# A last transpose moved from TensorE to DRAM, an earlier start and a closer order in a four-layer graph kernel

## Chip, cores and metric

One core of a Trainium2 chip. The metric is the device time of one execution in microseconds; every kernel here was run several times beside runs of the kernel before on the same chip. The experiments ran on three chips in turn, on which the kernel before took 1467.11, 1466.91 and 1466.23 us; so times from different groups may be compared to about 1 us. In the text PE is TensorE, DVE is VectorE, ACT is ScalarE, POOL is GpSimd and SP is SyncE, as in the profile.

## The reference, cut to what matters

```python
x = layernorm(x + attention_over_neighbours_0(x, adj, ...))      # layer 0
x = layernorm(x + attention_over_neighbours_1(x, adj, ...))      # layer 1
# layer 2: five gated steps; adj is symmetric and serves as both matrices
def step(h, _):
    m = einsum('nm,bmd->bnd', adj, h)                 # needs h with the nodes on the partitions
    u3 = h @ u3_w.T + u3_b                            # needs h with the features on the partitions
    z = sigmoid(av @ w3_w.T + w3_b + u3)              # av = [m, m]
    r = sigmoid(av @ w4_w.T + w4_b + u3)
    hv = tanh(av @ w5_w.T + w5_b + (r * h @ u5_w.T + u5_b))
    return (1 - z) * h + z * hv, None
x = layernorm(x + scan(step, x, length=5))
x = layernorm(x + chebyshev_3(x, adj, weight_1))                 # layer 3
```

`x` is 64 graphs x 256 nodes x 128 features, all float32. The kernel works on 32 units of two graphs.

Of the kernel before, what the change touches and what calls it, by code (L numbers as in the profile page):

```python
# [13 lines left out]
P = 128  # L14
# [6 lines left out]
BL = 32  # L21
NEAR = 1
DIRECT = 2


class Cell:
# [17 lines left out]
class Plan:  # L44
# [2 lines left out]



    LATENCY = {"pe": 700, "dve": 600, "act": 600, "pool": 700, "sp": 4000}  # L50
    OWN = {"pe": 0, "dve": 70, "act": 70, "pool": 100}

    def __init__(self, banks):
        self.free_banks = list(banks)
        self.tasks = []
        self.unit, self.step, self.layer = -1, 0, 0

    def add(self, eng, ns, fn, reads=(), writes=(), after=(), wait=0, group=None, dma=False):
        t = Task(eng, ns, fn, self.unit, wait, dma or eng == "sp")
        for c in reads:  # L60
            t.deps.update(c.writers)
            c.readers.append(t)
        for c in writes:
            if c.bank and not c.writers:
                t.takes.append(c)
            if group is None or c.group is not group:
                c.waits = {*c.writers, *c.readers} - {t}
                c.writers, c.readers, c.group = [], [], group
            t.deps.update(c.waits)
            c.writers.append(t)  # L70
        t.deps.update(after)
        t.deps.discard(t)
        for c in {id(c): c for c in (*reads, *writes) if c.bank}.values():
            c.users += 1
            t.banks.append(c)
        t.step = self.step = self.step + 1
        t.layer = self.layer
        self.tasks.append(t)
        return t

# [3 lines left out]
    def run(self, spawn, units, key):  # L84
# [32 lines left out]
        while any(ready.values()) or running:  # L117

            for t in [t for t in running if t.end <= now]:
                running.remove(t)  # L120
                for c in t.banks:
                    c.users -= 1
                    if not c.users:
                        self.free_banks.append(c.ap)
                open_units[t.unit] -= 1
                if not open_units[t.unit] and t.unit in lane_of:
                    start(lane_of[t.unit])
            for e, tasks in ready.items():
                if free[e] > now:
                    continue  # L130
                fit = [t for t in tasks if t.at <= now and len(t.takes) <= len(self.free_banks)]
                if not fit:
                    continue
                t = min(fit, key=key)
                tasks.remove(t)
                for c in t.takes:
                    c.ap = self.free_banks.pop(0)
                order.append(t)
                free[e] = t.off = now + t.ns
                t.end = t.off + self.LATENCY["sp" if t.dma else e] + t.wait  # L140
                done_at[t] = t.end
                running.append(t)
                for n in t.then:
                    n.left -= 1
                    n.at = max(n.at, self.seen_at(t, n))
                    if not n.left:
                        ready[n.eng].append(n)
            times = [t.end for t in running] + [f for f in free.values() if f > now]
            times += [t.at for tasks in ready.values() for t in tasks if t.at > now]
            times = [x for x in times if x > now]  # L150
            if not times:
                assert not any(ready.values()), "the plan is stuck"
                break
            now = min(times)
# [5 lines left out]
def kernel(  # L160
# [45 lines left out]
    def cell(name, shape):  # L206
        return Cell(sb(name, shape))
# [8 lines left out]
        return n * (cols * 1.667 + 5)  # L216


    def load(name, src, shape, ns=450):
        c = cell(name, shape)  # L220
        add("sp", ns, lambda: nc.sync.dma_start(c.ap, src), (), (c,))
        return c

    x_u = x.rearrange("(u b) (c p) d -> u p b c d", b=UB, p=P)
# [3 lines left out]

    zs = [cell(f"z{k}", [P, T]) for k in range(LANES)]

    def load_x(u):
        z = zs[u % LANES]
        if u < LANES:
            add("sp", 1000, lambda: nc.sync.dma_start(z.ap.rearrange("p (b c d) -> p b c d", b=UB, c=NC), x_u[u]), (), (z,))
            return
        parts = object()
        for a in range(D // BL):
            add("sp", 540, lambda a=a: nc.sync.dma_start(
                z.ap[a * BL : (a + 1) * BL].rearrange("j (b i) -> j b i", i=BL),
                x_a[u, a].rearrange("(b j) i -> j b i", j=BL)), (), (z,), group=parts)  # L240

    w1 = load("w1", W, [D, D])
    asd = cell("asd", [D, 2])
    for k, a in enumerate((a_src, a_dst)):
        add("sp", 450, lambda k=k, a=a: nc.sync.dma_start(asd.ap[:, k : k + 1], a), (), (asd,), group=asd)
    wo = load("wo", others_weight, [D, D])
    att = load("att", att_weight.rearrange("(k d) o -> d (k o)", k=2), [D, 2])
    load_x(0)
    wself = load("wself", self_weight, [D, D])
    adj_t = load("adj_t", adj.rearrange("(c p) j -> p c j", p=P), [P, NC, N])  # L250
    load_x(1)
    load_x(2)
    gates = [load(f"gate{k}", w.rearrange("o (s d) -> o s d", s=2), [D, 2, D])
             for k, w in enumerate((w3_w, w4_w, w5_w))]
    u3 = load("u3", u3_w, [D, D])
    u5 = load("u5", u5_w, [D, D])
    biases = cell("biases", [D, 5])
    for k, b in enumerate((w3_b, w4_b, w5_b, u3_b, u5_b)):
        add("sp", 450, lambda k=k, b=b: nc.sync.dma_start(biases.ap[:, k : k + 1], b.rearrange("(p o) -> p o", o=1)),
            (), (biases,), group=biases)  # L260
    load_x(3)
    wk = load("wk", weight_1, [D, D, 7], 1500)
    for u in range(4, LANES):
        load_x(u)


# [23 lines left out]
    for mc in range(NC):  # L290
# [2 lines left out]
                ps_adj.ap[:, mc * N + ic * P : mc * N + (ic + 1) * P], adj_t.ap[:, ic, mc * P : (mc + 1) * P], ident.ap),  # L293
                (adj_t, ident), (ps_adj,))
    add(ACT, 500, lambda: nc.scalar.copy(adjT.ap.rearrange("p c n -> p (c n)"), ps_adj.ap), (ps_adj,), (adjT,))

    adjTp, adj_p = cell("adjTp", [P, NC, N]), cell("adj_p", [P, NC * NC, BL, P // BL])
    add(DVE, 600, lambda: nc.vector.tensor_copy(
        adj_p.ap, adj_t.ap.rearrange("p i (m q j) -> p (i m) j q", m=NC, j=BL)), (adj_t,), (adj_p,))
    ps_adjp = bank()  # L300
    for mc in range(NC):
        for ic in range(NC):
            add(PE, 110, lambda mc=mc, ic=ic: nc.tensor.transpose(
                ps_adjp.ap[:, mc * N + ic * P : mc * N + (ic + 1) * P],
                adj_p.ap[:, ic * NC + mc].rearrange("p j q -> p (j q)"), ident.ap), (adj_p, ident), (ps_adjp,))
    add(ACT, 500, lambda: nc.scalar.copy(adjTp.ap.rearrange("p c n -> p (c n)"), ps_adjp.ap), (ps_adjp,), (adjTp,))
    neg0 = cell("neg0", [P, NC, N])
    add(DVE, 420, lambda: nc.vector.tensor_scalar(neg0.ap, adjT.ap, 0.0, NEG, op0=ALU.is_le, op1=ALU.mult),
        (adjT,), (neg0,))

    top0 = cell("top0", [P, NC])
    add(DVE, 350, lambda: nc.vector.tensor_reduce(top0.ap, neg0.ap[:, :, P:N], AX.X, ALU.max), (neg0,), (top0,))

    mask1 = cell("mask1", [P, NC, N])
    add(DVE, 420, lambda: nc.vector.tensor_copy(mask1.ap, adjT.ap), (adjT,), (mask1,))
    for c in range(NC):
        add(DVE, 250, lambda c=c: nc.vector.tensor_add(
            mask1.ap[:, c, c * P : (c + 1) * P], adjT.ap[:, c, c * P : (c + 1) * P], ident.ap),
            (adjT, ident, mask1), (mask1,))
    add(DVE, 420, lambda: nc.vector.tensor_scalar(mask1.ap, mask1.ap, 0.0, None, op0=ALU.is_gt), (mask1,), (mask1,))  # L320


    centre = cell("centre", [P, P])
    add(DVE, 150, lambda: nc.vector.tensor_scalar_add(centre.ap, ident.ap, -1.0 / D), (ident,), (centre,))
# [33 lines left out]
        add(DVE, 230, lambda t=t, n=n, ps=ps: nc.vector.tensor_copy(t.ap, ps.ap[:, 0:n]), (ps,), (t,))  # L358


    gs = [cell(f"gs{k}", [D, D]) for k in range(3)]
    for k in range(3):
        add(DVE, 250, lambda k=k: nc.vector.tensor_add(gs[k].ap, gates[k].ap[:, 0, :], gates[k].ap[:, 1, :]),
# [9 lines left out]
    add(DVE, 150, lambda: nc.vector.tensor_scalar_mul(bias2.ap[:, 0:2], bias2.ap[:, 0:2], 0.5), (bias2,), (bias2,))  # L373


    w3 = cell("w3", [D, 2, 2, D])
    add(DVE, 250, lambda: nc.vector.tensor_add(w3.ap[:, 0, 0, :], wk.ap[:, :, 0], ident.ap), (wk, ident), (w3,))
    for k in range(1, 4):
# [5 lines left out]
    for mc in range(NC):  # L384
        for kc in range(NC):
            add(PE, mm_ns(N), lambda mc=mc, kc=kc: nc.tensor.matmul(
                ps_a2.ap[:, mc * N : (mc + 1) * N], adj_t.ap[:, kc, mc * P : (mc + 1) * P], adjT.ap[:, kc, :],
                start=(kc == 0), stop=(kc == NC - 1)), (adj_t, adjT), (ps_a2,))
    add(DVE, 600, lambda: nc.vector.tensor_copy(a2T.ap.rearrange("p c n -> p (c n)"), ps_a2.ap), (ps_a2,), (a2T,))


    def lane_cells(k):
# [269 lines left out]
    def layer2(u, L):  # L662
        h, ht = turned(u, L), X[u]
        for step in range(STEPS):
# [39 lines left out]
            if step < STEPS - 1 and far(u):  # L704
# [8 lines left out]
                for a in range(D // BL):  # L713
# [2 lines left out]
                        L["hb"].ap[a * BL : (a + 1) * BL].rearrange("j (q g i) -> (j q) g i", g=G, i=BL)),  # L716
                        (L["hb"],), (ht,), group=parts)
                continue
            ps_t = bank()
            for g in range(G):  # L720
                add(PE, 110, lambda g=g, h=h, ps_t=ps_t: nc.tensor.transpose(  # L721
# [1 line left out]
            if step < STEPS - 1:  # L723
                add(ACT, 500, lambda ps_t=ps_t: nc.scalar.copy(L["ht"].ap, ps_t.ap), (ps_t,), (ht,))
        y = L["m"]
        add(DVE, 600, lambda: nc.vector.tensor_add(y.ap, ps_t.ap, X[u].ap.rearrange("p b c d -> p (b c d)")),
            (ps_t, X[u]), (y,))
        layernorm(u, L, y_pairs(y))


# [29 lines left out]
    def spawn(u, lane):  # L760
        for k, layer in enumerate((layer0, layer1, layer2, layer3)):
            plan.layer = k
            layer(u, lanes[lane])
            if not k and u + LANES < NU:
                load_x(u + LANES)



    def first(t):
        late = t.unit - (NU - LANES)  # L770
        if late >= 0 and t.layer > 1:
            return (1, t.step + late * LEAD)
        return (0, t.unit - (LANES if t.layer < 2 and t.unit >= LANES else 0))
# [34 lines left out]
```

## The kernel before: what the change touches

The kernel is written as a list of tasks. Each task names an engine, a duration that its author assumes (`ns`), what it reads and what it writes. A small planner then plays the program through with assumed durations and assumed latencies, and the order in which it picks the tasks becomes the order of instructions on each engine. The chip executes each engine's instructions in exactly that order. Seven units are in flight at a time, each in its own set of buffers, a "lane".

```python
LANES = 7
...
    LATENCY = {"pe": 700, "dve": 600, "act": 600, "pool": 700, "sp": 4000}     # assumed, ns
...
    # Plan.run: whenever an engine is free, among the tasks whose inputs have (by the plan) arrived
                t = min(fit, key=key)
                order.append(t)
                free[e] = t.off = now + t.ns
                t.end = t.off + self.LATENCY["sp" if t.dma else e] + t.wait
...
    def first(t):                                   # the key: the oldest unit first
        late = t.unit - (NU - LANES)
        if late >= 0 and t.layer > 1:
            return (1, t.step + late * LEAD)
        return (0, t.unit - (LANES if t.layer < 2 and t.unit >= LANES else 0))
```

The state `h` of a gated step is computed with the features on the partitions. After each step it must be turned. For 29 of the 32 units ("far" ones) the first four steps do that with a DVE transpose of 32x32 blocks and a trip through DRAM that moves the blocks; the last step uses four PE transposes for all units.

```python
            if step < STEPS - 1 and far(u):
                add(DVE, 600, lambda h=h, v=v: nc.vector.transpose(...), (h,), (v,))      # 32x32 blocks
                add("sp", 560, lambda v=v: nc.sync.dma_start(L["hb"].ap, v.ap), (v,), (L["hb"],))
                ...                                                   # four loads hb -> ht
                continue
            ps_t = bank()
            for g in range(G):
                add(PE, 110, lambda g=g, h=h, ps_t=ps_t: nc.tensor.transpose(
                    ps_t.ap[:, g * P : (g + 1) * P], h.ap[:, g * P : (g + 1) * P], ident.ap), (h, ident), (ps_t,))
            ...
        y = L["m"]
        add(DVE, 600, lambda: nc.vector.tensor_add(y.ap, ps_t.ap, X[u].ap...), (ps_t, X[u]), (y,))
```

The softmax here doesn't subtract the row's maximum and nothing guards it: scores larger than these inputs give would overflow.

## Time and profile before

| | kernel before |
|---|---|
| time, median of 3 | 1464.49 us (1464.2 to 1466.8) |
| profiled span | 1463.0 us, granted clock 0.992 |
| PE transposes of L721 | 176 of 128 columns, of them 116 in the last step of far units |
| DMA traffic | 126.90 MB |

These are the waits of PE in the full stretch from 100 to 1400 us of the kernel before: engine and line waiting, what it waited for, us in total, times, longest.

```profile
PE ps L678 <- ACT m L674: 3.6, 3, 1.8
PE ps L678 <- DVE xT L700: 3.1, 2, 1.9
PE ps L658 <- DMA ht<-hb: 1.5, 2, 1.3
```

The full list, two smaller waits included, comes to nine us of 1300. L678 is the gated products and L658 the product with the adjacency.

### The profile page before, as it was taken

How to read it: one execution, taken by the hardware profiler on the slowest of the kernel's cores; microseconds unless marked ns; L12 is line 12 of the kernel's file. 1: busy time of each engine (PE TensorE's matmuls, PEld its weight loads, DVE VectorE, ACT ScalarE, POOL GpSimd, SP SyncE). 2: the span in 40 equal slices, each digit the busy share in tenths (PEclk: the TensorE clock that was granted, in tenths of full speed). 3: DMA queues.
4: the chain of work that ended last, by engine and by line, in shares of the span. 5: the costliest groups of instructions: out<-in, count | busy, mean ns of one | idle time of the engine just before them, and what ended most of it. 6: DMA issues, size and time to landing. Idle time of an engine off the chain costs nothing.

```text
span 1463.0 us, 18345 instructions
## 1 busy us (share of the span) xinstructions
PE 1431.2 (98%) x5733; PEld 967.9 (66%) x5733; DVE 1101.1 (75%) x2569; ACT 723.2 (49%) x1372; POOL 146.2 (10%) x134
## 2 busy tenths in 40 slices
PE   7899999999999999999999999999999999999998
PEld 6666666666667766577666666676666766665667
DVE  6884778868769788777886778977976877767565
ACT  4664446446354465444554545535554554544431
POOL 0110101100011101001010011111100100001011
PEclk9899999999999999999999999999999999999999
DMA  6211243453534444534435344344343334443212
GB/s 148 46 37 22 65 96 86 95 110 78 116 80 95 104 98 87 118 74 99 104 80 108 78 109 100 84 92 107 72 98 85 89 89 99 93 101 70 46 44 65
DMA packets 495280, 126.90 MB, mean 87 GB/s; under 512 B 443856, under 2 KB 465104, under 8 KB 495184
## 3 DMA queue, kind: packets, MB, share of 16 engines
q1 hardware_dynamic: 495184, 125.73, 38.7%
q8 instruction: 46, 0.75, 0.2%
q14 instruction: 50, 0.41, 0.1%
HBM read 71.41 MB, written 54.25 MB: 86 GB/s over the span
## 4 chain that ended last, share of the span: by engine, by line
PE 93%; DVE 3%; ACT 2%; DMA 1%; issue 0%; SPq 0%; DVEq 0%; ACTq 0%
PE ps L678 45%; PE ps L658 22%; PE ps L747 8%; PE ps L754 4%; PE ps L620 3%; PE ps L590 3%; PE ps L523 2%; PE ps L634 2%; PE ps L585 2%; PE ps L721 1%; ACT e L609 1%; PE ps L430 0%; DVE e L554 0%; DVE st L483 0%; DMA rowu<-cu 0%
## 5 line engine op out<-in xcount | busy, mean ns | idle before, releaser
L678 PE MATMUL ps<-m,gT 128*128 128x512 f32 x960 | 460.9, 593 | 3.6 <-ACT m L674 3.6
L678 PEld LDWEIGHTS ps<-m,gT 128*128 128x128 f32 x960 | 177.7, 190 | 152.8 <-issue 126.4
L488 POOL TENSOR_TENSOR rstd<-ve,nhalf 128x4 f32<-128x4 f32 x128 | 145.5, 1139 | 1311.5 <-DVE ve L485 1268.9
L658 PE MATMUL ps<-adjTp,ht 128*128 128x256 f32 x928 | 231.7, 381 | 1.8 <-DMA ht<-hb 1.5
L658 PEld LDWEIGHTS ps<-adjTp,ht 128*128 128x128 f32 x928 | 174.5, 191 | 74.4 <-issue 50.1
L697 DVE TENSOR_TENSOR p<-p,xT 128x512 f32<-128x512 f32 x160 | 109.6, 686 | 95.3 <-ACT p L691 95.0
L674 ACT COPY m<-ps 128x512 f32<-128x512 f32 x160 | 93.4, 584 | 174.0 <-PE ps L658 170.1
L684 ACT ACTIVATE e<-ps,bias 128x512 f32<-128x512 f32 x160 | 109.8, 686 | 133.9 <-PE ps L678 133.8
L693 ACT ACTIVATE e<-ps,bias 128x512 f32<-128x512 f32 x160 | 109.7, 686 | 117.0 <-PE ps L678 116.7
L678 PE MATMUL ps<-xT,gT 128*128 128x512 f32 x320 | 161.4, 594 | 3.1 <-DVE xT L700 3.1
L686 DVE SCALAR_TENSOR_TENSOR e<-e,xT 128x512 f32<-128x512 f32 x160 | 109.2, 684 | 72.4 <-ACT e L684 70.9
L678 PE MATMUL ps<-e,u5T 128*128 128x512 f32 x320 | 161.9, 592 | 0.0
L691 ACT ACTIVATE p<-ps,bias 128x512 f32<-128x512 f32 x160 | 109.7, 686 | 77.9 <-PE ps L678 74.0
L658 PE MATMUL ps<-adjT,x 128*128 128x256 f32 x512 | 132.2, 383 | 0.0
L658 PEld LDWEIGHTS ps<-adjT,x 128*128 128x128 f32 x512 | 95.8, 192 | 42.6 <-issue 32.0
L698 DVE SCALAR_TENSOR_TENSOR p<-e,p 128x512 f32<-128x512 f32 x160 | 109.5, 685 | 2.8 <-ACT e L693 0.4
L700 DVE SCALAR_TENSOR_TENSOR xT<-p,xT 128x512 f32<-128x512 f32 x160 | 109.5, 685 | 2.0
L483 DVE BATCH_NORM_STATS2 st<-ps 128x6 f32<-128x256 f32 x128 | 53.7, 426 | 57.5 <-PE ps L754 38.9
L678 PEld LDWEIGHTS ps<-e,u5T 128*128 128x128 f32 x320 | 59.2, 190 | 51.1 <-issue 40.7
L609 ACT ACTIVATE e<-m,esd 128x256 f32<-128x256 f32 x120 | 87.0, 761 | 2.1 <-DMA m<-row 2.1
L678 PEld LDWEIGHTS ps<-xT,gT 128*128 128x128 f32 x320 | 59.1, 190 | 41.8 <-issue 31.0
L708 DVE STREAM_TRANSPOSE p<-xT 128x512 f32<-128x512 f32 x116 | 81.6, 705 | 1.4
(135 smaller groups left out, 1861.2 us busy)
## 6 DMA issues: line engine op xcount, KB each, us to landing
hb<-p SPq DMA_DIRECT2D x174, 256.0 KB, 2.1
ht<-hb SPq DMA_DIRECT2D x464, 64.0 KB, 2.5
m<-row SPq DMA_DIRECT2D x60, 256.0 KB, 3.7
xT<-hb SPq DMA_DIRECT2D x232, 64.0 KB, 2.5
out_dram<-x SPq DMA_DIRECT2D x32, 256.0 KB, 2.4
z<-in_x_dram SPq DMA_DIRECT2D x100, 64.0 KB, 2.4
z<-in_x_dram SPq DMA_DIRECT2D x7, 256.0 KB, 4.2
u<-rowu SPq DMA_DIRECT2D x60, 3.8 KB, 3.0
```

Of the source, the lines that this page charges most:

```text
L488: add(POOL, 1050, lambda: nc.gpsimd.tensor_tensor(rstd.ap, ve.ap, nhalf.ap, op=ALU.pow), (ve, nhalf), (rstd,))
L609: add(ACT, 600, lambda g=g, b=b: nc.scalar.activation(e.ap[:, g, :].rearrange("p (c n) -> p c n", c=NC), ev()[:, b], AF.Prelu, bias=esd.ap ...
L658: add(PE, mm_ns(N), lambda b=b, mc=mc: nc.tensor.matmul(ps.ap[:, b * N : (b + 1) * N], lhs(b, mc), mat.ap[:, mc, :], start=(mc == 0), stop ...
L678: add(PE, mm_ns(T), lambda: nc.tensor.matmul(ps.ap, w(), rhs.ap, start=start, stop=stop, skip_group_check=True), (c, rhs), (ps,))
L684: add(ACT, 600, lambda ps_g=ps_g: nc.scalar.activation(r.ap, ps_g.ap, AF.Tanh, bias=bias2.ap[:, 1:2], scale=0.5), (ps_g, bias2), (r,))
L686: add(DVE, 600, lambda h=h: nc.vector.scalar_tensor_tensor(r.ap, r.ap, 1.0, h.ap, op0=ALU.add, op1=ALU.mult), (r, h), (r,))
L691: add(ACT, 600, lambda ps_v=ps_v: nc.scalar.activation(v.ap, ps_v.ap, AF.Tanh, bias=bias2.ap[:, 2:3]), (ps_v, bias2), (v,))
L693: add(ACT, 600, lambda ps_g=ps_g: nc.scalar.activation(z.ap, ps_g.ap, AF.Tanh, bias=bias2.ap[:, 0:1], scale=0.5), (ps_g, bias2), (z,))
L697: add(DVE, 600, lambda h=h: nc.vector.tensor_sub(v.ap, v.ap, h.ap), (v, h), (v,))
L698: add(DVE, 600, lambda: nc.vector.scalar_tensor_tensor(v.ap, z.ap, 1.0, v.ap, op0=ALU.add, op1=ALU.mult), (v, z), (v,))
L700: add(DVE, 600, lambda h=h, new=new: nc.vector.scalar_tensor_tensor(new.ap, v.ap, 0.5, h.ap, op0=ALU.mult, op1=ALU.add), (v, h), (new,))
L747: add(PE, mm_ns(N), lambda k=k, src=src, c=c, b=b: nc.tensor.matmul(view(c)[:, :, b, :], bn(src.ap)[:, b, c * P : (c + 1) * P], w3.ap[:, k ...
```

## The change

Its intent has three parts, called here the last step (L), the start (S) and the closer order (C).

L: the last step's state of a far unit also goes through DRAM, in natural token order, and the final addition reads it from SBUF.

```diff
+            if far(u):
+                add(DVE, 600, lambda h=h, v=v: nc.vector.transpose(...), (h,), (v,))
+                parts = object()
+                for a in range(D // BL):
+                    add("sp", 560, lambda a=a, v=v: nc.sync.dma_start(
+                        L["hb"].ap.rearrange("(q j) (a r) -> a j q r", j=BL, a=D // BL)[a],
+                        v.ap[a * BL : (a + 1) * BL].rearrange("j (q r) -> j q r", q=P // BL)), (v,), (L["hb"],), group=parts)
+                add("sp", 450, lambda: nc.sync.dma_start(ht.ap, L["hb"].ap), (L["hb"],), (ht,))
+                continue
             ps_t = bank()
...
-        add(DVE, 600, lambda: nc.vector.tensor_add(y.ap, ps_t.ap, X[u]...), (ps_t, X[u]), (y,))
+        if far(u):
+            add(DVE, 600, lambda: nc.vector.tensor_add(y.ap..., ht.ap..., X[u].ap...), (ht, X[u]), (y,))
+        else:
+            add(DVE, 600, lambda: nc.vector.tensor_add(y.ap, ps_t.ap, X[u]...), (ps_t, X[u]), (y,))
```

S: first loads in another order, the adjacency and unit 1's input issued from ACT; constants that the first unit doesn't need are moved behind those that it does, with a rank in the key; and the first prefetches get a rank. The durations assumed for some first loads change with it (1000 and 1500 ns become 600).

```diff
     w1 = load("w1", W, [D, D])
+    adj_t = load("adj_t", adj.rearrange("(c p) j -> p c j", p=P), [P, NC, N], by=ACT)
+    load_x(0)
+    wo = load("wo", others_weight, [D, D])
...
-    adj_t = load("adj_t", adj.rearrange("(c p) j -> p c j", p=P), [P, NC, N])
-    load_x(1)
+    load_x(1, ACT)
...
+    plan.rank = 0        # ... R2, R3 for groups of constants; u + LANES for prefetches
...
+        if t.rank is not None:
+            return (0, t.rank)
```

C: the planner assumes shorter latencies, still shorter ones in the first 35 us.

```diff
-    LATENCY = {"pe": 700, "dve": 600, "act": 600, "pool": 700, "sp": 4000}
+    LATENCY = {"pe": 500, "dve": 400, "act": 400, "pool": 500, "sp": 4000}
+    EARLY = {"pe": 250, "dve": 180, "act": 200, "pool": 250, "sp": 2500}
...
-                t.end = t.off + self.LATENCY["sp" if t.dma else e] + t.wait
+                t.end = t.off + (self.EARLY if now < START else self.LATENCY)["sp" if t.dma else e] + t.wait
```

More of the change, by code (lines that the diff above doesn't have):

```diff
@@ L23 @@
 DIRECT = 2
+START = 35e3
+R2 = 1
+R3 = 1.5
 class Cell:
@@ L56, in __init__ @@
         self.unit, self.step, self.layer = -1, 0, 0
+        self.rank = None
     def add(self, eng, ns, fn, reads=(), writes=(), after=(), wait=0, group=None, dma=False):
@@ L77, in add @@
         t.layer = self.layer
+        t.rank = self.rank
         self.tasks.append(t)
@@ L216, in mm_ns, with load @@
         return n * (cols * 1.667 + 5)
-    def load(name, src, shape, ns=450):
+    def load(name, src, shape, ns=450, by="sp"):
         c = cell(name, shape)
-        add("sp", ns, lambda: nc.sync.dma_start(c.ap, src), (), (c,))
+        queue = {"sp": nc.sync, ACT: nc.scalar}[by]
+        add(by, ns, lambda: queue.dma_start(c.ap, src), (), (c,), dma=True)
         return c
@@ L229, with load_x @@
     zs = [cell(f"z{k}", [P, T]) for k in range(LANES)]
-    def load_x(u):
+    def load_x(u, by="sp"):
         z = zs[u % LANES]
         if u < LANES:
-            add("sp", 1000, lambda: nc.sync.dma_start(z.ap.rearrange("p (b c d) -> p b c d", b=UB, c=NC), x_u[u]), (), (z,))
+            queue = {"sp": nc.sync, ACT: nc.scalar}[by]
+            add(by, 600, lambda: queue.dma_start(z.ap.rearrange("p (b c d) -> p b c d", b=UB, c=NC), x_u[u]), (), (z,), dma=True)
             return
@@ L245 @@
         add("sp", 450, lambda k=k, a=a: nc.sync.dma_start(asd.ap[:, k : k + 1], a), (), (asd,), group=asd)
-    wo = load("wo", others_weight, [D, D])
     att = load("att", att_weight.rearrange("(k d) o -> d (k o)", k=2), [D, 2])
-    load_x(0)
     wself = load("wself", self_weight, [D, D])
-    adj_t = load("adj_t", adj.rearrange("(c p) j -> p c j", p=P), [P, NC, N])
-    load_x(1)
+    load_x(1, ACT)
     load_x(2)
@@ L256 @@
     u5 = load("u5", u5_w, [D, D])
+    load_x(3)
     biases = cell("biases", [D, 5])
@@ L260 @@
             (), (biases,), group=biases)
-    load_x(3)
-    wk = load("wk", weight_1, [D, D, 7], 1500)
-    for u in range(4, LANES):
+    load_x(4)
+    wk = load("wk", weight_1, [D, D, 7], 600)
+    for u in range(5, LANES):
         load_x(u)
@@ L295 @@
     add(ACT, 500, lambda: nc.scalar.copy(adjT.ap.rearrange("p c n -> p (c n)"), ps_adj.ap), (ps_adj,), (adjT,))
-    adjTp, adj_p = cell("adjTp", [P, NC, N]), cell("adj_p", [P, NC * NC, BL, P // BL])
-    add(DVE, 600, lambda: nc.vector.tensor_copy(
-        adj_p.ap, adj_t.ap.rearrange("p i (m q j) -> p (i m) j q", m=NC, j=BL)), (adj_t,), (adj_p,))
-    ps_adjp = bank()
-    for mc in range(NC):
-        for ic in range(NC):
-            add(PE, 110, lambda mc=mc, ic=ic: nc.tensor.transpose(
-                ps_adjp.ap[:, mc * N + ic * P : mc * N + (ic + 1) * P],
-                adj_p.ap[:, ic * NC + mc].rearrange("p j q -> p (j q)"), ident.ap), (adj_p, ident), (ps_adjp,))
-    add(ACT, 500, lambda: nc.scalar.copy(adjTp.ap.rearrange("p c n -> p (c n)"), ps_adjp.ap), (ps_adjp,), (adjTp,))
     neg0 = cell("neg0", [P, NC, N])
@@ L312 @@
     add(DVE, 350, lambda: nc.vector.tensor_reduce(top0.ap, neg0.ap[:, :, P:N], AX.X, ALU.max), (neg0,), (top0,))
-    mask1 = cell("mask1", [P, NC, N])
-    add(DVE, 420, lambda: nc.vector.tensor_copy(mask1.ap, adjT.ap), (adjT,), (mask1,))
-    for c in range(NC):
-        add(DVE, 250, lambda c=c: nc.vector.tensor_add(
-            mask1.ap[:, c, c * P : (c + 1) * P], adjT.ap[:, c, c * P : (c + 1) * P], ident.ap),
-            (adjT, ident, mask1), (mask1,))
-    add(DVE, 420, lambda: nc.vector.tensor_scalar(mask1.ap, mask1.ap, 0.0, None, op0=ALU.is_gt), (mask1,), (mask1,))
     centre = cell("centre", [P, P])
@@ L358 @@
         add(DVE, 230, lambda t=t, n=n, ps=ps: nc.vector.tensor_copy(t.ap, ps.ap[:, 0:n]), (ps,), (t,))
+    plan.rank = 0
+    mask1 = cell("mask1", [P, NC, N])
+    add(DVE, 420, lambda: nc.vector.tensor_copy(mask1.ap, adjT.ap), (adjT,), (mask1,))
+    for c in range(NC):
+        add(DVE, 250, lambda c=c: nc.vector.tensor_add(
+            mask1.ap[:, c, c * P : (c + 1) * P], adjT.ap[:, c, c * P : (c + 1) * P], ident.ap),
+            (adjT, ident, mask1), (mask1,))
+    add(DVE, 420, lambda: nc.vector.tensor_scalar(mask1.ap, mask1.ap, 0.0, None, op0=ALU.is_gt), (mask1,), (mask1,))
+    plan.rank = R2
     gs = [cell(f"gs{k}", [D, D]) for k in range(3)]
@@ L373 @@
     add(DVE, 150, lambda: nc.vector.tensor_scalar_mul(bias2.ap[:, 0:2], bias2.ap[:, 0:2], 0.5), (bias2,), (bias2,))
+    adjTp, adj_p = cell("adjTp", [P, NC, N]), cell("adj_p", [P, NC * NC, BL, P // BL])
+    add(DVE, 600, lambda: nc.vector.tensor_copy(
+        adj_p.ap, adj_t.ap.rearrange("p i (m q j) -> p (i m) j q", m=NC, j=BL)), (adj_t,), (adj_p,))
+    ps_adjp = bank()
+    for mc in range(NC):
+        for ic in range(NC):
+            add(PE, 110, lambda mc=mc, ic=ic: nc.tensor.transpose(
+                ps_adjp.ap[:, mc * N + ic * P : mc * N + (ic + 1) * P],
+                adj_p.ap[:, ic * NC + mc].rearrange("p j q -> p (j q)"), ident.ap), (adj_p, ident), (ps_adjp,))
+    add(ACT, 500, lambda: nc.scalar.copy(adjTp.ap.rearrange("p c n -> p (c n)"), ps_adjp.ap), (ps_adjp,), (adjTp,))
+    plan.rank = R3
     w3 = cell("w3", [D, 2, 2, D])
@@ L389 @@
     add(DVE, 600, lambda: nc.vector.tensor_copy(a2T.ap.rearrange("p c n -> p (c n)"), ps_a2.ap), (ps_a2,), (a2T,))
+    plan.rank = None
     def lane_cells(k):
@@ L718, in layer2 @@
                 continue
+            if far(u):
+                add(DVE, 600, lambda h=h, v=v: nc.vector.transpose(
+                    v.ap.rearrange("p (q g i) -> p g q i", g=G, i=BL), h.ap.rearrange("p (g q j) -> p g q j", g=G, j=BL)),
+                    (h,), (v,))
+                parts = object()
[5 more added lines that the diff above has]
+                continue
             ps_t = bank()
@@ L725, in layer2 @@
         y = L["m"]
-        add(DVE, 600, lambda: nc.vector.tensor_add(y.ap, ps_t.ap, X[u].ap.rearrange("p b c d -> p (b c d)")),
-            (ps_t, X[u]), (y,))
+        if far(u):
+            add(DVE, 600, lambda: nc.vector.tensor_add(
+                y.ap.rearrange("p (g a i) -> p g a i", g=G, i=BL), ht.ap.rearrange("p (a g i) -> p g a i", g=G, i=BL),
+                X[u].ap.rearrange("p b c (a i) -> p (b c) a i", i=BL)), (ht, X[u]), (y,))
+        else:
+            add(DVE, 600, lambda: nc.vector.tensor_add(y.ap, ps_t.ap, X[u].ap.rearrange("p b c d -> p (b c d)")),
+                (ps_t, X[u]), (y,))
         layernorm(u, L, y_pairs(y))
@@ L764, in spawn @@
             if not k and u + LANES < NU:
+                plan.rank = u + LANES if u < LANES else None
                 load_x(u + LANES)
+                plan.rank = None
     def first(t):
+        if t.rank is not None:
+            return (0, t.rank)
         late = t.unit - (NU - LANES)
```

## The prediction

> **What bounds the kernel now.** I read the page first (busy shares, slices, the chain that ended last), then busy time by stage, then PE's waits, then PE in order of time.
>
> ```profile
> PE 1431.2 (98%) x5733; PEld 967.9 (66%) x5733; DVE 1101.1 (75%) x2569; ACT 723.2 (49%) x1372; POOL 146.2 (10%) x134
> PE   7899999999999999999999999999999999999998
> PE 93%; DVE 3%; ACT 2%; DMA 1%; issue 0%; SPq 0%; DVEq 0%; ACTq 0%
> ```
>
> PE is busy for 98% of the span and makes up 93% of the chain; only the first two slices (and the last) fall short. So time comes off in two ways only: fewer PE instructions, or less time lost before PE is full. A busy PE need not be at its peak, so I did not rest on the share. I took start-to-start distances from the order in time: a 512-column record is 0.43 us after the last, a 256-column one 0.216, a 128-column transpose 0.11. Counting the records of each stage by form and multiplying gives 21.1 us of work in the first 31 us (9.9 lost), 15.6 in 31 to 63 us (16.4 lost), 1378.5 in 63 to 1456.4 (14.9 lost in 1393), and then 6.6 us after the last matmul. Lost time is thus 26 us at the start, about 1% in the middle, and 7 at the end.
>
> ```profile
> 0.00:31.00 31.00, 25.48 (x189) 24.10 (x189) 18.32 (x75) 14.86 (x42) 1.72 (x7) 1.00 0.68 155
> 31.00:63.00 32.00, 21.43 (x115) 18.38 (x116) 31.08 (x106) 17.09 (x51) 5.66 (x5) 0.73 0.31 63
> 100.00:1400.00 1300.00, 1290.92 (x5015) 855.55 (x5014) 986.32 (x2225) 648.53 (x1199) 123.02 (x108) 1.00 0.40 89
> ```
>
> The columns are PE, PEld, DVE, ACT and POOL busy time, then the granted clock, DMA share and GB/s. In the second stage DVE is full (31.08 of 32 us), PE waits for it, and PE's clock is down to 0.73. In the long third stage PE is full and DVE has a quarter of its time free.
>
> The start, in PE's waits of the first 63 us and the chain:
>
> ```profile
> PE ps L430 <- DVE x L497: 4.7, 1, 4.7
> PE ps L473 <- DVE esd L595: 4.2, 2, 3.2
> PE ps L327 <- DMA w<-in_L_gnn_W_dram: 2.8, 1, 2.8
> ...
> 4.13 3.84 DMA adj_t<-in_adj_dram
> 28.22 2.72 DMA u<-rowu
> 37.22 3.63 DMA m<-row
> ```
>
> The adjacency is the eighth load on SP, issued at 4.13 us and landed at 7.97. DVE stands behind it (its copy adj_p waits for it), PE stands behind it too, and from there PE runs without a gap to about 27 us. Then a row of unit 2 goes through DRAM, late because SP had 12 prefetches of 0.74 us each to issue ahead of it (the row starts at 22.63 us, its input was ready at about 20).
>
> **What the Trainium skill says.** (1) "TensorE: Matmul & The Clock Gate", Part 4: PE-mode transpose: it is the only path that transposes a full 128x128 in one shot, its output goes to PSUM, and one takes some 275 ns in a kernel. The trace agrees with the duration (273 ns), but back to back, or between matmuls, it takes 0.11 us of PE's time, and that is what I charge. (2) The same page, Part 1: after a window of about 3.4 us of idleness PE falls to half clock until it has been busy for such a window. The trace agrees: the transposes at 56.84 us, after a gap of 4.65 us, last 0.42 to 0.48 us instead of 0.27, and eight records of L620 at 38.79 us last 3.78 us instead of 1.89. A gap at the start costs more than itself. (3) "VectorE: DVE Perf Modes", The three transpose paths: DVE's transpose does 32x32 blocks only, so a full one needs something that moves the blocks; here DMAs through DRAM. In this trace one over 128x512 takes 705 ns. (4) "DMA: Bandwidth & Descriptors", Issuing engines are not separate DMA queues: a load issued from ACT saves the sequencer's issue time and gives no bandwidth. No run shows this yet (before issues all from SP).
>
> **The change part by part.**
>
> ```profile
> L721 PE MATMUL ps<-ident,xT 128*128 128x128 f32 x176 | 31.3, 273 | 0.0
> L708 DVE STREAM_TRANSPOSE p<-xT 128x512 f32<-128x512 f32 x116 | 81.6, 705 | 1.4
> L726 DVE TENSOR_TENSOR m<-ps,x 128x512 f32<-128x512 f32 x32 | 22.0, 688 | 20.9 <-PE ps L721 20.9
> hb<-p SPq DMA_DIRECT2D x174, 256.0 KB, 2.1
> ht<-hb SPq DMA_DIRECT2D x464, 64.0 KB, 2.5
> ```
>
> Last step. There are 32 units of 2 graphs; 29 of them (2 to 30) take the new way. Removed: 4 transposes each, 116 of the 176 of L721. 116 x 0.11 = 12.8 us of PE, nearly all where PE is full (the first would fall after 100 us; six units lie in the last 70 us, where PE is full to 1456). Added on DVE: 29 x 0.70 = 20 us, so 75% becomes 77%, beside PE. The final addition reads SBUF in place of PSUM, same elements: unchanged. Added on SP: 4 issues of about 0.6 us and one of 0.45, 29 x 2.9 = 83 us; from counts and durations SP issues for some 620 of 1463 us now, so it goes to about half. Added traffic: 29 x 512 KB = 15 MB on 127, in runs of 512 B and more (some 18 thousand packets on 495 thousand). DMA share goes from 39% to perhaps 41%. All of this is beside PE. Latency added to a unit: transpose 0.7, four issues 2.4, landing 2.1, issue and landing 2.6: 8 us against 1, in a unit that lives about 320 us (1463 x 7 lanes / 32). With seven units in flight that is hidden, except at the end. Net: -12.5 us.
>
> Start. The adjacency becomes ACT's first issue, so it lands near 4.7 us (0.75 + 3.8) rather than 8.0. But the instruction order of the changed kernel puts about 5 us of DVE constants ahead of the copy of wx0, which the first real products need, so these products start near 10.3 us, as before (10.1), with the constants' and the squared adjacency's work already done: about 1.5 us of PE ahead. SP has two loads fewer and 10 prefetches instead of 12 ahead of the first row: that row goes 2 to 3 us earlier. In the DVE-full stretch, summing the row durations in DVE's order up to the last instruction that starts unit 0's gated layer gives 42.4 us of DVE against 44.9. I take the gated layer to start 4 to 6 us before 57 us, of which some may be lost again to gaps: -4.5 us.
>
> Closer order. The scheduler's assumed latencies fall from 600 to 700 ns to 400 to 500 ns (200 to 250 early). From the trace, ACT starts 0.03 us after a modelled end of PE, that is about 0.2 us after the end of PE's issue, and DVE and ACT results are seen some 0.1 to 0.2 us late, so the assumptions still leave room in the middle. What can change is the 14.9 us lost there: I give it 0, plus or minus 6.
>
> End. Unit 30 leaves through the DRAM hops now. From its last gate on, before had some 27 us of PE work queued and needed about 13 us of latency; the new path needs about 20 us and then 5 of products, 25 in all. Just hidden, so +1.
>
> Sum: 1464.5 - 12.5 - 4.5 + 0 + 1 = 1448.5 us (-1.1%).
>
> **The rivals.** (a) The start gains nothing, because DVE is full from 31 to 63 us whatever lands first, and the order built on 180 to 250 ns exposes waits of PE. For it: wx0 is no earlier. Against it: unit 0's path is 2.5 us of DVE shorter. Then 1452 to 1454. (b) The closer order turns into waits in the full stretch: ACT activations of L609 last 761 ns where the plan says 600, and the read of an accumulator costs 193 ns more at L568, so ACT and DVE drift behind the plan and PE, in order, waits. For it: PE already waits there now and then. Against it: 200 to 300 ns of room remain, and other lanes have work. If each of 160 steps lost 0.1 us it would be +16, so 1464, no gain. (c) The end is stretched by the two DRAM hops: unit 30's path is not hidden, +5 to +7; then 1454. (d) The better order cures more than I think: start -10, middle -8, with the transposes 1434. The losses of 26 and 15 us allow that; the DVE-full start speaks against it.
>
> **Range and chances.** The 12.5 us are firm to 1 us. The start has a spread of 4, the middle of 6, the end of 3; together about 8 either way: 1438 to 1458. Faster by over 2% needs less than 1435.2 us, which only (d) reaches: 0.09. Slower needs +29 us: 0.01. Within 2%: 0.90.
>
> **What would show it.** Right: L721's successor has 60 transposes instead of 176; DVE has 29 more transposes of about 0.7 us and is at 76 to 78%; PE's busy time falls by some 12 to 17 us; the adjacency lands before 5 us; the first gated product of unit 0 starts near 57 us instead of 62.7; lost PE time between there and the end stays at about 15 us. Wrong: more and longer waits of PE for ACT, DVE or ht in the middle (b), a gap of PE ahead of the last unit's products after 1430 us (c), or a gated layer that still starts at 60 us or later (a).

## The result, and the profile after

The changed kernel takes 1451.59 us (median of 4 runs, 1449.94 to 1453.05) against 1465.47 us of the kernel before in the same rounds: 13.9 us less, inside the predicted range and 3 us above the predicted time. The ratio is 0.9905, 95% interval 0.9887 to 0.9922. All outputs are right. Here and below a ratio is the mean time of one kernel's runs over the mean of the other's runs of the same rounds, so it is not quite the ratio of the medians quoted.

The profile's page of the kernel after, its busy line, PE's slices and the chain by engine:

```profile
PE 1416.8 (98%) x5617; PEld 952.5 (66%) x5617; DVE 1116.6 (77%) x2598; ACT 724.5 (50%) x1372; POOL 144.8 (10%) x134
PE   7899999999999999999999999999999999999998
...
PE 92%; DVE 4%; ACT 2%; DMA 1%; issue 1%; SPq 1%; POOLq 0%; POOL 0%; DVEq 0%; ACTq 0%
```

PE has 116 instructions less and 14.4 us less of busy time; DVE went from 75 to 77%; and the first two slices are no fuller. The groups that replace L721 and the addition of before, in the costliest groups by form (busy us, mean ns of one, idle time before them):

```profile
L738 DVE STREAM_TRANSPOSE p<-xT 128x512 f32<-128x512 f32 x29 | 20.5, 707 | 0.4
L756 DVE TENSOR_TENSOR m<-ht,x 128x512 f32<-128x512 f32 x29 | 19.7, 680 | 2.5 <-PE ps L637 2.2 <-DMA ht<-hb 0.2
...
L750 PE MATMUL ps<-ident,xT 128*128 128x128 f32 x60 | 11.1, 273 | 0.0
```

And the new trips through DRAM in the list of DMA issues (KB each, us from issue to landing):

```profile
hb<-p SPq DMA_DIRECT2D x116, 64.0 KB, 1.8
ht<-hb SPq DMA_DIRECT2D x29, 256.0 KB, 2.9
```

DVE waited 0.2 us in all for these landings. So far each line is as the prediction had it. The stages, with the columns as in the prediction's table of stages:

```profile
0.00:31.00 31.00, 24.86 (x193) 23.85 (x193) 20.61 (x89) 16.09 (x47) 1.95 (x8) 1.00 0.65 148
31.00:63.00 32.00, 20.76 (x109) 16.15 (x110) 27.97 (x90) 17.17 (x54) 4.18 (x4) 0.84 0.38 70
100.00:1400.00 1300.00, 1292.65 (x4976) 853.82 (x4975) 1013.76 (x2285) 655.34 (x1208) 125.66 (x111) 1.00 0.45 101
```

In the second stage DVE is less full than before (27.97 us for 31.08) and PE's clock is higher (0.84 for 0.73). The first gated product of unit 0 starts at 59.00 us in place of 62.67. Yet PE's useful work changed little, because the time moved into other waits. The waits of PE in the first 63 us of the kernel after:

```profile
PE ps L490 <- DVE esd L612: 5.4, 2, 5.1
PE ps L303 <- DMA adj_t<-in_adj_dram: 4.2, 1, 4.2
PE ps L447 <- DVE x L514: 3.4, 1, 3.4
```

And two pieces of the chain in order of time there (start us, us):

```profile
0.73 3.38 DMA adj_t<-in_adj_dram
...
29.87 4.36 DMA u<-rowu
```

The adjacency landed at 4.11 us in place of 7.97, but PE's first instruction now waits for it until 4.2 us, where PE had begun at 2.8 us before. And the waits for scores (esd), two of 4.2 us in all before (the longest 3.2), are now two of 5.4 us, with 5.1 us for unit 1's: DVE, in order, stood 2.5 us at an instruction of unit 3 that waited for a row whose trip took 4.36 us.

To say where time went, the same accounting as in the prediction was done for every run: records of each form times their start-to-start distance is PE's work, and the rest of a stretch is lost time. It is good to about 1 us. The middle here runs from 63 us to 62.8 us before the end of the span.

| lost PE time, us | first 63 us | middle | last 62.8 us |
|---|---|---|---|
| before | 26 | 14 | 6 |
| after | 25 | 14 | 7 |

The work itself fell from 1416 to 1403 us. So nearly all of the gain is the transposes; the start gave some 2 us (1.7 before rounding); the rest is unchanged. That reading leaves three equal-looking theories: L alone gives the gain; the three parts add up; or the parts depend on each other. The runs decide.

### The profile page after: what moved, and what is told of

Read it like the earlier page. It is cut to its first block, busy times and chain, and to the rows that moved or that the text cites. A ratio compares the mean times of both kernels' runs of the same rounds, so it can differ in the third digit from the quotient of the medians.

```text
span 1448.2 us, 18393 instructions
## 1 busy us (share of the span) xinstructions
PE 1416.8 (98%) x5617; PEld 952.5 (66%) x5617; DVE 1116.6 (77%) x2598; ACT 724.5 (50%) x1372; POOL 144.8 (10%) x134
## 2 busy tenths in 40 slices
DMA packets 516162, 142.12 MB, mean 98 GB/s; under 512 B 446176, under 2 KB 482272, under 8 KB 516064
## 4 chain that ended last, share of the span: by engine, by line
PE 92%; DVE 4%; ACT 2%; DMA 1%; issue 1%; SPq 1%; POOLq 0%; POOL 0%; DVEq 0%; ACTq 0%
PE ps L695 45%; PE ps L675 22%; PE ps L781 8%; PE ps L637 4%; PE ps L788 4%; PE ps L607 3%; PE ps L540 2%; PE ps L651 2%; PE ps L602 2%; DMA u<-rowu 0%; PE ps L750 0%; ACT p L585 0%; DVE st L500 0%; PE ps L447 0%; ACT e L626 0%
## 5 line engine op out<-in xcount | busy, mean ns | idle before, releaser
L675 PE MATMUL ps<-adjT,x 128*128 128x256 f32 x512 | 127.7, 379 | 0.0
L500 DVE BATCH_NORM_STATS2 st<-ps 128x6 f32<-128x256 f32 x128 | 53.7, 426 | 54.8 <-PE ps L788 44.3
```

The source lines that it names most:

```text
L675: add(PE, mm_ns(N), lambda b=b, mc=mc: nc.tensor.matmul(ps.ap[:, b * N : (b + 1) * N], lhs(b, mc), mat.ap[:, mc, :], start=(mc == 0), stop ...
```

## The experiments

### One part alone

Three kernels were made from the kernel before, each with one part of the change, and one control. Edits: `last_only` has the diff of L above and nothing else; `start_only` that of S; `close_only` that of C. The control:

```diff
-    LATENCY = {"pe": 700, "dve": 600, "act": 600, "pool": 700, "sp": 4000}
+    LATENCY = {"pe": 700, "dve": 600, "act": 600, "pool": 700, "sp": 4200}     # reshuffle
```

> The kernel before with the last step alone changed (116 PE transposes away; loads, constants and latencies as before). Theory: 116 x 0.11 us = 12.8 us of PE come off, so -11 to -13 us against before, and PE's busy time falls by as much. Rival (c), the DRAM hops of the last units stretch the end: -6 or less, with a gap of PE after 1420 us. Rival 'the gain is the better order': near 0.

> The kernel before with the loads and constants reordered and ranked alone (latencies and last step as before). The prediction gave the start as a whole -4.5 us; the profile after shows only 1.7 us less lost time in the first 63 us. Theory: -1 to -3 us. Rival: the reorder alone is worth 4 to 6 us and the tighter early latencies gave it back: -4 to -6.

> The kernel before with the smaller assumed latencies alone. Theory: lost time in the middle stays near 11 us, so 0 plus or minus 3. Rival (b): PE waits more for ACT and DVE, +5 or more. Rival (d): the closer order cures gaps, -5 or more.

> The kernel before with only the planner's assumed DMA landing changed from 4000 to 4200 ns: the same work in another order, with no intent. It measures how far a mere re-dealing of the order moves the time. Theory: within 3 us of before. If it moves by 5 us or more, single parts of a few us cannot be read from single kernels.

Measured against 1467.1 us of the kernel before in these rounds: `last_only` 1486.91 us, ratio 1.0135 (1.0122 to 1.0149), so 19.8 us slower; `start_only` 1467.29 us, 1.0000 (0.9988 to 1.0013); `close_only` 1469.58 us, 1.0017 (1.0005 to 1.003); `reshuffle` 1468.51 us, 1.001 (0.9996 to 1.0024).

The part that removes 12.7 us of PE work makes the kernel 20 us slower when it comes alone, and no part alone gains anything. The theory that the parts add up is dead: 19.8 + 0 + 2.5 is not -13.9. In `last_only` the work fell by 13 us as it should, but the loss in the middle rose from 14 to 47 us. PE's busy time, which was expected to fall with the work, did not (1431.4 us for 1431.2): work is a count of instructions times a fixed distance, while busy time also holds records that follow each other late. The one reshuffled order was 1.4 us slower than the kernel before; no such control was run on a kernel with L.

The adjacency landed at 4.05 us in `start_only`, and the first gated product still started at 64.64 us, later than before. So an earlier landing, in this order, was worth nothing.

### All but one part

Three kernels were made from the kernel after, each with one part undone: `no_last` without the diff of L, `no_start` with the old loads, constants and key, `no_close` with the old latencies and no `EARLY`. A fourth tests the 5.1 us wait at its start.

```diff
-    EARLY = {"pe": 250, "dve": 180, "act": 200, "pool": 250, "sp": 2500}
+    EARLY = {"pe": 250, "dve": 180, "act": 200, "pool": 250, "sp": 4500}       # late_dma
```

> The changed kernel with its last step back on PE (reordered start and closer latencies kept). Theory: some 12 us slower than the changed kernel, so -1 to -3 us against before. Rival (the reorder does most of it): -8 or more against before.

> The changed kernel with loads and constants in the old order and no ranks (last step and closer latencies kept). Theory: start worth about 2 us, so -11 to -13 us against before. If the reordered start carries 4.5 us as predicted: -9 to -10.

> The changed kernel with the old latencies (600 to 700 ns, no early ones). Theory: within 2 us of the changed kernel, so -12 to -16 against before. Rival (b), the closer order costs: faster than the changed kernel by 3 us or more.

> The changed kernel with one number changed: the early assumed DMA landing is 4500 ns instead of 2500. In DVE's order unit 3's d, which waited 2.5 us for its row, then stands behind unit 1's normalisation instead of ahead of it. Theory (the start's predicted gain was lost to DVE standing behind a row that lands late): unit 1's esd is ready by about 32 us instead of 35, PE's wait of 5.1 us there shrinks to about 2, and the time falls by 1 to 4 us against the changed kernel (-15 to -18 against before). Rival (DVE is full there whatever the order): unit 1's esd comes earlier but the gated layer starts no earlier, 0 plus or minus 1.5.

Measured against 1466.9 us: `no_last` 1466.83 us, ratio 1.0001 (0.9989 to 1.0013); `no_start` 1467.6 us, 1.0006 (0.9992 to 1.0019); `no_close` 1474.71 us, 1.0059 (1.0045 to 1.0073); `late_dma` 1482.39 us, 1.0105 (1.009 to 1.0121).

`late_dma` did locally less than it was made for: DVE now stood 1.6 us at a row ahead of unit 1's esd in place of 2.5, PE's wait there shrank from 5.1 to 3.9 us (about 2 was foreseen), and the first 63 us lost 24 us in place of 25. But the kernel became 31 us slower than the kernel after, and all of it in the middle, for instance 13 us lost between 400 and 600 us, long after the first 35 us in which the changed number applies. That number shifts the first picks, and every later pick follows from those. So the start's waits are not what the time hangs on. My theory of a gain of 1 to 4 us fell as well, and the rival (0 plus or minus 1.5) with it.

By now a pattern was to be seen. Kernels with the PE transposes lay within 0 to +2.5 us, whatever the order. Kernels with the trip through DRAM ran from -14 to +20 us. Two explanations were left. Hardware: the trips cost time on the chip (landings that are waited for, SP's queue, the round of the buffers). Order: the trips are hidden on the chip, but the planner, which books each DMA at 4 us and more (2.5 us in the first 35 us where C is present), makes a worse order out of them. An example of what such an order does is in `last_only`; its SP timeline (start us, us, line, what):

```profile
728.16 0.34 SPq L729 DMA_DIRECT2D ht<-hb  x1
740.25 0.40 SPq L775 DMA_DIRECT2D out_dram<-x  x1
746.52 1.92 SPq L238 DMA_DIRECT2D z<-in_x_dram  x4
...
755.69 1.27 SPq L539 DMA_DIRECT2D u<-rowu  x2
757.02 1.92 SPq L449 DMA_DIRECT2D xT<-hb  x3
```

SP stood for 11.7 us at a store whose data DVE had not finished, then for 5.8 us at a prefetch, and then issued almost without a pause from 746.5 us on. The loads of xT that PE needed were among them, and PE waited 4.1 us for the last one. No trip was slow in this; the issues stood in line. But this shows what happened, not why.

### Order or hardware

```diff
-    LATENCY = {"pe": 700, "dve": 600, "act": 600, "pool": 700, "sp": 4000}     # in last_only
+    LATENCY = {"pe": 700, "dve": 600, "act": 600, "pool": 700, "sp": 2500}     # last_near_dma
```

```diff
-    LATENCY = {"pe": 500, "dve": 400, "act": 400, "pool": 500, "sp": 4000}     # in the kernel after
+    LATENCY = {"pe": 500, "dve": 400, "act": 400, "pool": 500, "sp": 2500}     # after_near_dma
```

```diff
 # in the kernel before: the PE transposes stay, but the plan believes that their result comes 8 us late
                 add(PE, 110, lambda g=g, h=h, ps_t=ps_t: nc.tensor.transpose(
-                    ...), (h, ident), (ps_t,))
+                    ...), (h, ident), (ps_t,), wait=8000 if step == STEPS - 1 and far(u) else 0)   # believe_slow
```

```diff
-LANES = 7
+LANES = 6                                                                       # six_lanes, in the kernel before
```

> The last-step change alone, as in last_only, with one number more: the planner is told that a DMA issued by SyncE takes 2500 ns instead of 4000. The instructions, the bytes and the rotating buffers are those of last_only; only the order in which they are issued differs. Theory (the plan's belief about the two added trips through DRAM spoils its order: the trips land in 1.8 to 2.9 us but were planned at 4 us each and more): the 33 us of TensorE time that last_only lost beyond the kernel before go away for the most part, and the run comes to -8 to -14 us against the kernel before (ratio 0.990 to 0.9945). Rival (the trips themselves, SyncE's queue and the round of buffers cost the time on the chip): it stays at +10 to +22 us (ratio 1.007 to 1.015).

> The changed kernel with the planner's SyncE latency at 2500 ns. Theory (belief): it is at least as good as the changed kernel, -13 to -20 us against the kernel before (ratio 0.9865 to 0.991). Rival (real landings come later than the plan then believes, and TensorE waits for them; or the order of the changed kernel is a lucky one among orders that scatter): 0 to +10 us (ratio 1.000 to 1.007).

> The kernel before, with its TensorE transposes of the last step and not one transfer more; only the planner is told that these transposes give their result 8 us late. The instructions are those of the kernel before in another order. If the plan's belief is what cost last_only its 33 us, this one is slower as well, +5 to +25 us against the kernel before (ratio 1.003 to 1.017). If the cost is in the transfers and queues themselves, it stays within 3 us (ratio 0.998 to 1.002).

> The kernel before with six units in flight instead of seven; the work is the same. If seven units are barely enough to fill TensorE (a unit's own chain lasts about 300 us, 7 units by 43.8 us of TensorE work are 307 us), then six give 6 x 43.8 = 263 us of work for a chain of 300 us, and the middle grows by up to a seventh: +40 to +150 us (ratio 1.03 to 1.10). If there is slack in the number of units, as the prediction took for granted, it is within 5 us (ratio 0.997 to 1.004).

Measured against 1466.23 us of the kernel before:

| run | median, us | ratio | 95% interval |
|---|---|---|---|
| last_near_dma | 1449.38 | 0.9885 | 0.9871 to 0.99 |
| after_near_dma | 1459.09 | 0.995 | 0.9932 to 0.9968 |
| believe_slow | 1479.85 | 1.0093 | 1.008 to 1.0107 |
| six_lanes | 1505.81 | 1.0275 | 1.026 to 1.029 |

`last_near_dma` has the same tasks as `last_only`, as many instructions on PE, DVE, ACT and POOL (5617, 2598, 1372, 134) and the same 142.12 MB of traffic. It is 37.5 us faster. Nothing but the order, and with it which free buffer or bank a tile gets, differs. The rival that the trips as such cost the 33 us on the chip is dead. The PE waits of `last_only` from 100 to 1400 us:

```profile
PE ps L678 <- DVE xT L700: 8.8, 10, 2.0
PE ps L678 <- ACT m L674: 4.9, 5, 2.1
PE ps L764 <- DMA xT<-hb: 4.1, 1, 4.1
PE ps L590 <- DVE h L572: 2.8, 2, 2.3
PE ps L658 <- DMA ht<-hb: 2.6, 4, 1.4
PE ps L678 <- DVE e L686: 1.9, 1, 1.9
```

The same view of `last_near_dma`:

```profile
PE ps L658 <- DMA ht<-hb: 3.5, 4, 1.6
PE ps L678 <- ACT m L674: 0.7, 1, 0.7
PE ps L678 <- DVE xT L700: 0.4, 1, 0.4
```

The waits that went away are those for DVE and ACT results (L700, L674, L686, L572) and the one 4.1 us wait that stood in SP's line; those for landings of ht did not shrink. The waits of these two views come to 29 and 5 us in full, the losses to 47 and 10: some 13 us of the difference are not waits but lie between records that follow each other late. In the stretch from 700 to 900 us, for one, PE's granted clock was 0.98 in `last_only` and 1.00 in `last_near_dma`. The final addition, which is what really waits for the new trip, in the groups by form of `last_only`:

```profile
L739 DVE TENSOR_TENSOR m<-ht,x 128x512 f32<-128x512 f32 x29 | 19.7, 678 | 3.2 <-DMA ht<-hb 3.0
```

and of `last_near_dma`:

```profile
L739 DVE TENSOR_TENSOR m<-ht,x 128x512 f32<-128x512 f32 x29 | 19.9, 686 | 10.1 <-DMA ht<-hb 9.7 <-PE ps L678 0.4
```

DVE waits three times as long for the trip in the fast kernel as in the slow one. That fits a plan that expects the landing sooner, and PE lost no time by it (10 us in the middle), for DVE is busy for 77% of the span only. The chain that ended last says the same; by engine, `last_only`:

```profile
PE 82%; DVE 11%; DMA 3%; ACT 2%; SPq 1%; issue 1%; DVEq 0%; ACTq 0%
```

and `last_near_dma`:

```profile
PE 90%; DVE 4%; DMA 2%; SPq 2%; ACT 1%; issue 1%; DVEq 0%
```

`believe_slow` is the same test from the other side. No transfer and no instruction was added, only a belief, and it is 13.6 us slower; its middle lost 26 us for 14. This order, made for a late result, is worse on a chip where the result is early. It does not reach `last_only`'s 47 us, so one late result per unit of that size is not the whole of what the plan did there.

`six_lanes` lost 55 us in the middle in place of 14 and came out 39.6 us slower, just below the range of my theory and far outside that of the rival. With six lanes PE's own work is 6 x 44.3 = 266 us per round (1416 us of work over 32 units is 44.3; the expectation had taken the 43.8 of the kernels with L). 41 us more over 32 / 6 = 5.3 rounds are 8 us per round, so by this estimate a unit's chain lasts some 275 us. Against 7 x 44.3 = 310 us that leaves some 35 us of room with seven lanes: enough for the 7 us that the two trips add, not enough to give a lane away. The estimate takes all of the 41 us for a lack of units; six lanes also make another order, and what part of the loss is that, no run separates. My statement that seven lanes are barely enough was too strong, and the prediction's, that the trips are hidden by seven units in flight, holds on the chip in the order of `last_near_dma`.

`after_near_dma` missed. It was to be at least as good as the kernel after, and gains 7 us instead of 14; its rival (0 to 10 us slower than the kernel before) missed as well. In the profiled run, its slowest, 25 us were lost in the middle. Its runs spread more, too (1454.82 to 1463.48, with one and the same order). So 2500 ns is no rule: it made a good order of one task list and a mediocre one of another.

All runs together (L, S, C: the parts present; lost PE time in us as above; ratio to the kernel before of the same rounds). The ratio is of all runs, the lost time of the profiled one alone, which for `after` was the fastest of four and for `after_near_dma` the slowest of six:

| run | parts | ratio | first 63 | middle | last 62.8 |
|---|---|---|---|---|---|
| before | none | 1 | 26 | 14 | 6 |
| reshuffle | none, SP 4200 ns | 1.001 | 28 | 16 | 6 |
| start_only | S | 1.0000 | 28 | 14 | 6 |
| close_only | C | 1.0017 | 26 | 21 | 7 |
| no_last | S, C | 1.0001 | 24 | 17 | 7 |
| believe_slow | none, belief | 1.0093 | 28 | 26 | 8 |
| six_lanes | none, six lanes | 1.0275 | 27 | 55 | 6 |
| last_only | L | 1.0135 | 28 | 47 | 7 |
| no_close | L, S | 1.0059 | 27 | 35 | 7 |
| no_start | L, C | 1.0006 | 23 | 31 | 7 |
| after | L, S, C | 0.9905 | 25 | 14 | 7 |
| late_dma | L, S, C, early SP 4500 ns | 1.0105 | 24 | 48 | 7 |
| after_near_dma | L, S, C, SP 2500 ns | 0.995 | 28 | 25 | 6 |
| last_near_dma | L, SP 2500 ns | 0.9885 | 28 | 10 | 6 |

The middle column moves most (10 to 55 us, the first by 5 and the last by 2), and with L the ratio follows it. The best version is `last_near_dma`: L and one number, without S and C. Its interval overlaps that of the kernel after, so the two are not told apart, and both beat the kernel before by about 1%.

## Why the prediction was right, and where it was not

The sum was right to 3 us of 1464, by steps that were not all right: in part it was luck.

**Last step, -12.5 us.** The removal is right: 60 transposes are left, PE's work fell by 13 us in every kernel with L, DVE went to 77%, the trips landed in 1.8 and 2.9 us. The words "All of this is beside PE" and "With seven units in flight that is hidden" hold on the chip in a fitting order, as `last_near_dma` shows: ratio 0.9885 with L alone, and no more lost time than before. They do not hold for this kernel's own planner at the numbers of before: there L costs 33 us of PE time and comes to +19.8.

**Closer order, 0 plus or minus 6.** This is the step that failed. I looked for what the shorter assumed latencies could cure in the 14.9 us lost in the kernel before, and found nothing to cure, which is right: `close_only` and `no_last` gain nothing. But C doesn't meet the kernel before, it meets a kernel with L. Without C, with L and S, the kernel is at 1.0059, with it at 0.9905: in that company it is worth 22 us. I valued each part against the kernel before and added; the parts do not add. The middle lost 14 us before and after because C and S happened to bring an order that fits L, and not because nothing happened there. That the sum came out is luck in this term.

**Start, -4.5 us.** Mis-sized: by the accounting it gave some 2 us in the kernel after. The adjacency landed before 5 us, as foreseen, and the gated layer began at 59.00 us, 3.7 us earlier where 4 to 6 were. But the time of the gated layer's start was the wrong measure. Other units' work fills PE before it, and PE waited longer for esd. The earlier gated layer goes with the shorter latencies of the first 35 us rather than the loads: it starts at 64.64 us in `start_only`, at 60.73 us in `close_only` and at 58.05 us in `no_start`, which has the old loads. The long wait for esd goes with S: the longest is 4.4 us in `start_only` and in `no_last`, and 2.8 us in `close_only` and in `no_start`. And 23 to 28 us are lost at the start in every run, the fastest included. Like C, S is worth more in company: without it, with L and C, the kernel is at 1.0006, so 15 us slower than with it, and the loss is in the middle (31 us for 14), far from the loads that S moves.

**End, +1 us.** The last stretch lost 7 us for 6, which is within the accuracy of the accounting; PE had no wait after 1380 us. Right, as far as this shows.

**Rivals.** (a) came nearest with its number (1452 to 1454), but not by its reason alone: DVE was less full than before (27.97 us for 31.08), and the time went into waits. (b) named the danger, an order that turns into waits in the full stretch, but put it on the wrong part: I feared that C makes waits, and L makes them where C is missing. (c) and (d) did not come to pass.

**Small slips.** 0.75 + 3.8 is 4.55 and not 4.7 (the adjacency landed at 4.11 us). "4 to 6 us before 57 us" should read "4 to 6 us before 62.7 us, near 57", as its last paragraph has it. The DMA share went to 0.44, not 0.41.

What stays open: why one assumed latency gives a good order and a neighbouring one a bad one. The runs show that the order decides and that beliefs about latency shift the time by up to 37.5 us. They don't give a rule for choosing the numbers, and they don't show whether 2500 ns is good in `last_near_dma` because it is nearer to the landings or by chance, since no neighbouring value was tried beside it: among the seven kernels with L the results scatter from 0.9885 to 1.0135, and the two with 2500 ns differ by 10 us.

## What to carry to other kernels

Where a planner, a priority or an assumed latency decides the order, parts of a change do not add up: after adding a step of long latency, look at the assumed latency of that step first, try a value near what the trace shows (here landings of 1.8 to 2.9 us for an assumed 4; it gained 37.5 us in `last_only` and lost 7 in the kernel after), and try a few orders before judging the step. To separate order from hardware, run the same tasks in another order, and the old tasks in an order made for the new latency; two runs (`last_near_dma` and `believe_slow`) settled here what the eight before them could not. And the lost time must be looked for in the long full stretch too: 33 us more in 1300 moved PE's busy share only from 98 to 96%; the waits showed 20 of them, the distances between starts all.

## What the Trainium skill lacked or had wrong

- Belongs to "DMA: Bandwidth & Descriptors", Rules for kernel authors, where it is said that a DMA issued early and waited for late has its fixed cost overlapped. True of the chip here (`last_near_dma`, DVE waits 9.7 us in all for 29 new trips, PE no more than before), but the page has no word on the order of the other instructions, which decided between ratios of 1.0135 and 0.9885 with the same transfers.
- Belongs to the same page, Issuing engines are not separate DMA queues, which the prediction uses. The page's statement that only issue time is saved is not contradicted: with two loads issued from ACT the core moved 148 GB/s in the first 31 us, for 155 before. What it lacks is whether neighbours land later. The small loads did: att 3.7 us after its issue for 2.2 before, the pair asd 3.9 to 4.2 us for 2.1 to 2.2. But unit 0's input was also moved ahead of them on SP, so the runs don't tell which of the two delayed them.
- Belongs to the same page: what one waiting issue costs the issues behind it on the same engine's queue. SP stood 11.7 us at one store and then issued a burst, and PE waited 4.1 us for a load in it (`last_only`), although the landing itself took 2.5 us.
- Belongs to "TensorE: Matmul & The Clock Gate", Part 4, which gives a transpose's duration only: 116 of them, each 273 ns long in the trace, took 13 us of PE's work, 0.11 us each from start to start. The duration would have put it at 32 us.
